# Down projections with slots on the output partitions, and experts' slots in tiles of six and four, in a macaron block of experts and attention

## The chip, the cores and the metric

The kernel runs on one core of one Trainium2 chip. The metric is the device time of one execution, in microseconds (us); lower is better. The profiles are of one execution each, taken by the hardware profiler. In them PE is TensorE (PEld its weight loads), DVE is VectorE, ACT is ScalarE, POOL is GpSimd and SP is SyncE. L12 is line 12 of the kernel file.

## The reference

x has 4 x 2048 rows (tokens) of D = 256 f32 values. The block is a "macaron": half a mixture-of-experts layer, an attention layer, and half a mixture-of-experts layer again, each on the normalized rows and added to x.

```python
x = x + 0.5 * ffn(layernorm(x), router_w, wg, wu, wd)
x = x + attn(layernorm(x), Wq, bq, Wk, bk, Wv, bv, Wo, bo)
x = x + 0.5 * ffn(layernorm(x), router_w, wg, wu, wd)

def ffn(x, router_w, wg, wu, wd):              # E = 8 experts, K = 2 of them per token, F = 1024
    capacity = int(1.25 * N / E)               # 1280 slots per expert
    topw, topi = top_k(softmax(x @ router_w.T), K)
    ...                                        # each expert keeps its `capacity` heaviest tokens
    g = einsum('ecd,edf->ecf', disp, wg)       # disp: the kept tokens' rows
    u = einsum('ecd,edf->ecf', disp, wu)
    eo = einsum('ecf,efd->ecd', silu(g) * u, wd)
    out = zeros.at[token].add(eo * weight)     # back to the tokens, scaled
```

The attention is linear: a softmax over the 16 features of each head of q, a softmax of that over the tokens for k, a context per head, and the projection Wo. Its work is not touched by the change.

## The kernel before, in words

**Stages.** The program runs through: the first router (layer norm statistics, logits, choice of two experts, a bisection for each expert's threshold, up to 96 us in the profile), the first phase of experts (to about 892 us), attention (to about 1100), the second router's threshold (to about 1169), and the second phase of experts (to the end). A phase of experts is a call of `experts`.

**An expert.** Each has 1280 slots, ten tiles of 128. Before the change they are worked in two chunks of CH = 5 tiles, 16 chunks k in a phase; k even is an expert's first chunk, k odd its second. For each chunk: `gather` fetches the rows by indirect DMAs from GpSimd's queue, one for each tile, into tiles `r`; `norm` applies the layer norm on ScalarE (L625); `turn` transposes the rows on TensorE (L636, `tr`), so that D lies on the partitions, and ScalarE copies them out (L639, `xsT`). Then `units` makes the gate and up products and `down` the down projection.

**Strassen–Winograd.** Both `units` and `down` use the seven-product scheme for a 2 x 2 block product in place of eight products. In `units` the blocks are the halves of D, the halves of F, and the halves of the slots (BH = 320 columns each). F's half is worked in NF = 4 units p of 128; each unit has seven products for the gate (m = 0) and for the up weights (m = 1), all at L701. The weights' sums `ws` are made per expert by `weight_sums` (L588), the rows' sums `xs` by `sums_of_x`. VectorE adds the products up from PSUM (L642), ScalarE takes the silu (L729, L751), and the product silu(g) * u is `finish` (L732), on VectorE for p = 0, 1 and 3 and on GpSimd for p = 2. `sums_of_h` then makes the sums of the hidden blocks that the down products need, on GpSimd (L645) for p = 0, 1 and 2 and on VectorE for p = 3. `h(p)` and `hT(p)` name the hidden blocks and their sums; they lie with F on the partitions and slots along the free dimension.

**The down projection.** `down` makes seven products over four p each (L912). In each call a 128 x 128 block of the down weights, or of their sums `wds`, is the stationary operand and 320 slots of the hidden state move, so the result has D on the partitions:

```python
nc.tensor.matmul(ps, a(p), b(p), start=(p == 0 and not more), stop=(p == NF - 1), skip_group_check=more)
```

In the call the second argument is stationary and the third moves. The result `y` must come back to slots on the partitions: `send` transposes it on TensorE (L864, `back`), ScalarE scales each row by its routing weight into a buffer `eo` (L845), and GpSimd issues one indirect DMA per tile that adds the rows into the output in DRAM (L846). A phase's last chunk takes `down_at_once` (L973): eight plain products for each tile, hidden tile stationary, 256 weight columns moving, no transposes.

**Order.** Inside `experts` the order on TensorE, VectorE, ScalarE and SP is the order in which the code issues (`tc.manual_schedule`); GpSimd's is chosen by the framework's scheduler. Work of the next chunk and expert is put between the products by hand: `early` and `late` (called in unit p of `units`), `next_list` (the row list of the next expert, made during an even chunk from 64 small products at L535 whose operands ScalarE makes at L529), `sums_of_w` (the next expert's `ws`, on VectorE during an odd chunk's `down`), and `sum_of_wd`. `gather(k + 1)` is issued in unit 0 of an odd chunk, `gather(k + 2)` in its `down`. PSUM accumulators come from `banks()`, three buffers of two banks each, reused in turn. In `down`, c11 is the first product's accumulator, p1 its copy, and u2 and u3 are partial sums.

Of the kernel before, what the change touches and what calls it, by code (L numbers as in the profile page):

```python
# [27 lines left out]
def macaron_kernel(  # L28
# [31 lines left out]
    CH = 5  # L60
# [416 lines left out]
    class RowList:  # L477
# [12 lines left out]
        def high(self):  # L490
            hi = self.pool.tile([P, T * HI], F16, tag="hi", name="hi", bufs=1)
            hv = self.pool.tile([P, 2 * T * HI], F16, tag="hv", name="hv", bufs=1)
            at = slot_hi[:, self.e, :]
            if self.waited_for:
                shape = [P, HI, T // TG, TG]
# [10 lines left out]
            else:  # L506
                shape, hi = [P, T, HI], hi.rearrange("p (t i) -> p t i", i=HI)
# [3 lines left out]
                self.hv = hv.rearrange("p (t k i) -> p t k i", k=2, i=HI)  # L511
                nc.vector.tensor_scalar(self.hv[:, :, 0, :], hi, row_in, None, ALU.mult)
                nc.vector.tensor_tensor(self.hv[:, :, 1, :], hi, spread(row_of.unsqueeze(2), shape), ALU.mult)

# [57 lines left out]
    BH = CH * P // 2  # L572
    TURN = 3
# [17 lines left out]
    def experts(name, src, dst, wait_for, rest, weights, ws, wpool, lpool, pool, ppool):  # L591
# [4 lines left out]
        PER = ST // CH  # L596
        NL = T // TG
        assert PER == 2 and ST % CH == 0
        chunks = [(e, i) for e in range(E) for i in range(0, ST, CH)]
        lists, got, xTs, turned, wds, xs = {}, {}, {}, {}, {}, {}  # L600
        sent, gathers = {-1: list(wait_for)}, {}

        def gather(k):
# [4 lines left out]
            for i in range(i0, i0 + CH):  # L608
                r = lpool.tile([P, W], F32, tag="r", name="r", bufs=10)
                gathers[k].append(nc.gpsimd.indirect_dma_start(  # L610
                    out=r, out_offset=None, in_=src[:, :],
                    in_offset=bass.IndirectOffsetOnAxis(ap=lists[e][:, i : i + 1], axis=0),
                ))
                got[k].append(r)
# [12 lines left out]
        def turn(k, q):  # L627

            if k >= len(chunks):
                return  # L630
            if q == 0:
                turned[k] = xTs[k] = pool.tile([P, DC, CH * P], F32, tag="xsT", name="xsT", bufs=2)
            c, i0, i1 = q // 2, (0, TURN)[q % 2], (TURN, CH)[q % 2]
# [13 lines left out]
        def sums_of_w(e, m):  # L647
            for _ in weight_sums(nc.vector, e, wpool, weights, ws, m):
                pass
# [25 lines left out]
        def sums_of_x(k):  # L675
            if k >= len(chunks):
                return
            v = turned.pop(k)
            o = xs[k] = pool.tile([P, 4, BH], F32, tag="xs", name="xs", bufs=1)
# [10 lines left out]
        def units(k):  # L690
            e = chunks[k][0]
# [42 lines left out]
            def first_product(p):  # L734

                ps = both(p, 0, 0, xT[:, 0, :BH])
                p1 = pool.tile([P, 2, BH], F32, tag="p1", name="p1", bufs=1)
# [3 lines left out]
            def sixth_product(p):  # L741
# [13 lines left out]
            if k == 0:  # L755

                turn(0, 1)
                cts[0] = pool.tile([P, 2, 4, BH], F32, tag="ct", name="ct", bufs=NF)
# [15 lines left out]
            send(k - 1, 2, 3)  # L774
# [67 lines left out]
        def send_tile(k, i, ps):  # L842
            e, i0 = chunks[k]
            eo = pool.tile([P, D], F32, tag="eo", name="eo", bufs=5)
            nc.scalar.mul(eo, ps, got[k][i][:, D + e : D + e + 1])  # L845
# [3 lines left out]
                in_=eo, in_offset=None, compute_op=ALU.add,  # L849
# [6 lines left out]
        def send(k, *tiles):  # L856
# [3 lines left out]
            y = ys[k]  # L860
            ps = ppool.tile([P, BANK], F32, tag="tr", name="back", bufs=1)
            for n, i in enumerate(tiles):
                for j in range(DC):
                    nc.tensor.transpose(  # L864
                        ps[:, n * D + j * P : n * D + (j + 1) * P], y[:, j, i * P : (i + 1) * P], ident
                    )
# [17 lines left out]
        def late(k, p):  # L884

            if p == 0:
                send(k - 1, 4)
# [606 lines left out]
```

## Time and profile before

| | us |
|---|---|
| median of 3 runs | 1972.2 (1971.08 to 1973.48) |
| profiled execution, its own time | 1971.7 |
| its span, from first to last instruction | 1969.7 |
| TensorE busy | 1843.7 |
| VectorE busy | 1337.3 |
| ScalarE busy | 1039.1 |
| GpSimd busy | 1027.3 |
| first phase of experts, from 96 to 892 us: TensorE busy | 784.3 of 796 |
| second phase of experts, from 1169 to 1969 us: TensorE busy | 779.4 of 800 |

How to read the profile: "busy" is the time in which at least one instruction of the engine runs. Matmuls overlap each other in the array, so the mean duration of one is longer than the distance from one start to the next; that distance is called pitch below. A line of groups reads: code line, engine, operation, output <- inputs, shape, count | busy us, mean ns of one | idle us of the engine just before them, with who ended most of that idle time. A line of the chain or of the timeline begins with the start and the length in us. The granted TensorE clock is full in the two phases of experts, except at their starts.

### The profile page before, as it was taken

The numbers are of one execution on the slowest core, as the hardware profiler recorded it, in microseconds if no ns is written. First come the engines' busy times: TensorE is split into PE (matmuls) and PEld (weight loads), VectorE is DVE, ScalarE is ACT, GpSimd is POOL, SyncE is SP. The second block draws the span as 40 slices with busy tenths as digits, with TensorE's granted clock in tenths as the row PEclk, the third lists the DMA queues.
The fourth block names the chain that finished last, engine by engine and source line by source line (L and its number), as shares of the span: only waits on it lengthen the run. The fifth ranks groups of instructions, "written<-read, shape, count | busy, mean of one in ns | idle before, by whom it ended". The sixth has DMA issues, their size and how long they took to land.

```text
span 1969.7 us, 25694 instructions
## 1 busy us (share of the span) xinstructions
PE 1843.7 (94%) x8840; PEld 1333.2 (68%) x8840; DVE 1337.3 (68%) x2445; ACT 1039.1 (53%) x2647; POOL 1027.3 (52%) x1003
## 2 busy tenths in 40 slices
PE   7389999999999999999999639999999999999998
PEld 5256677777777777777888526667777777777776
DVE  7766767676767676646677667776666767676763
ACT  5676555454646463325666368473737373737332
POOL 5245555555555555535555433555555555555552
PEclk9599999999999999999999859999999999999999
DMA  9822222222222221115012540222232313131121
GB/s 336 278 93 71 50 71 50 71 50 71 50 71 50 72 50 29 28 22 179 22 43 90 200 158 5 71 50 71 50 75 47 88 33 95 28 96 28 31 28 19
DMA packets 108002, 148.87 MB, mean 76 GB/s; under 512 B 7512, under 2 KB 94560, under 8 KB 107872
## 3 DMA queue, kind: packets, MB, share of 16 engines
q1 hardware_dynamic: 76992, 103.16, 15.3%
q0 software_dynamic: 30720, 43.93, 13.6%
q8 instruction: 70, 1.15, 0.2%
q10 hardware_dynamic: 160, 0.14, 0.1%
q14 instruction: 60, 0.49, 0.1%
HBM read 91.11 MB, written 56.10 MB: 75 GB/s over the span
## 4 chain that ended last, share of the span: by engine, by line
PE 47%; DVE 4%; issue 1%; ACT 1%; POOL 1%; DMA 1%; POOLq 0%; ACTq 0%; SPq 0%; DVEq 0%
PE mm L701 24%; PE mm L912 10%; PE py L1227 3%; PE pc L1169 3%; PE qp L1110 2%; PE back L864 1%; PE tr L636 1%; PE trq L1157 1%; PE ix L535 1%; PE trx L1102 1%; DVE above L431 1%; DVE cand L438 0%; DVE ct L642 0%; POOL out_dram L846 0%; DMA xw<-acc 0%
## 5 line engine op out<-in xcount | busy, mean ns | idle before, releaser
L701 PE MATMUL mm<-xs,ws 128*128 128x320 f32 x1536 | 477.6, 433 | 2.9 <-DVE u L642 1.8
L645 POOL TENSOR_TENSOR ct<-ct 128x320 f32<-128x320 f32 x360 | 340.4, 945 | 189.1 <-DVE ct L732 165.6
L701 PEld LDWEIGHTS mm<-xs,ws 128*128 128x128 f32 x1536 | 284.0, 190 | 112.0 <-DVE u L642 2.8
L642 DVE TENSOR_TENSOR ct<-u,mm 128x640 f32<-128x640 f32 x256 | 209.8, 820 | 177.6 <-PE mm L701 146.7
L610 POOL DMA_INDIRECT r<-rows,ixs x160 | 156.7, 980 | 280.6 <-ACT eo L845 182.1
L729 ACT ACTIVATE ct<-ct 128x960 f32<-128x960 f32 (+2 forms) x192 | 141.7, 738 | 281.9 <-DVE ct L642 276.4
L642 DVE TENSOR_TENSOR ct<-ct,mm 128x640 f32<-128x640 f32 x288 | 235.9, 819 | 74.0 <-PE mm L701 69.8
L912 PE MATMUL mm<-ct,wds 128*128 128x320 f32 x960 | 278.8, 433 | 3.4 <-DVE y L642 2.1
L529 ACT ACTIVATE lo<-from_below,behind_lo 128x129 f16<-128x129 f32 x896 | 272.9, 395 | 0.0
L912 PEld LDWEIGHTS mm<-ct,wds 128*128 128x128 f32 x960 | 179.1, 190 | 76.8 <-DVE ct L642 3.5
L912 PE MATMUL mm<-ct,wdt 128*128 128x320 f32 x720 | 213.9, 433 | 0.0
L846 POOL DMA_INDIRECT out_dram<-eo,ixs x80 | 128.5, 1606 | 144.9 <-ACT eo L845 127.0
L846 POOL DMA_INDIRECT acc<-eo,ixs x80 | 127.6, 1596 | 145.2 <-ACT eo L845 127.2
L701 PE MATMUL mm<-xsT,wgt 128*128 128x320 f32 x512 | 185.9, 445 | 0.1
L701 PE MATMUL mm<-xsT,wut 128*128 128x320 f32 x512 | 180.7, 435 | 0.0
L732 DVE TENSOR_TENSOR ct<-ct 128x640 f32<-128x640 f32 (+1 forms) x128 | 159.8, 1248 | 21.8 <-ACT ct L729 21.8
L912 PEld LDWEIGHTS mm<-ct,wdt 128*128 128x128 f32 x720 | 131.8, 190 | 47.4 <-issue 0.3
L642 DVE TENSOR_TENSOR u<-p,mm 128x640 f32<-128x640 f32 x128 | 105.1, 821 | 83.0 <-PE mm L701 66.1
L701 PE MATMUL mm<-xsT,ws 128*128 128x320 f32 x512 | 159.5, 434 | 0.0
L738 ACT COPY p<-mm 128x640 f32<-128x640 f32 x128 | 88.2, 689 | 131.5 <-PE mm L701 129.6
L845 ACT ACTIVATE eo<-back,r 128x256 f32<-128x256 f32 x150 | 64.8, 477 | 137.0 <-PE back L864 134.2
L701 PEld LDWEIGHTS mm<-xsT,wut 128*128 128x128 f32 x512 | 97.7, 191 | 40.7 <-issue 0.8
(299 smaller groups left out, 2881.8 us busy)
## 6 DMA issues: line engine op xcount, KB each, us to landing
wgt<-in_L_ffn_wg_dram SPq DMA_DIRECT2D x16, 1024.0 KB
wut<-in_L_ffn_wu_dram SPq DMA_DIRECT2D x16, 1024.0 KB
wdt<-in_L_ffn_wd_dram SPq DMA_DIRECT2D x16, 1024.0 KB
rows<-xw SPq DMA_DIRECT2D x6, 2240.0 KB
xw<-in_L_attn_x_dram SPq DMA_DIRECT2D x16, 512.0 KB
acc<-xw SPq DMA_DIRECT2D x4, 2048.0 KB
out_dram<-xw SPq DMA_DIRECT2D x16, 512.0 KB
xw<-acc SPq DMA_DIRECT2D x15, 512.0 KB
```

The source lines that it names most:

```text
L529: nc.scalar.activation(lo[:, t, :], from_below, AF.Sign, bias=at, scale=1.0)
L610: gathers[k].append(nc.gpsimd.indirect_dma_start(out=r, out_offset=None, in_=src[:, :], in_offset=bass.IndirectOffsetOnAxis(ap=lists[e][:, ...
L642: nc.vector.tensor_tensor(o, a, b, op)
L645: nc.gpsimd.tensor_tensor(o, a, b, op)
L701: nc.tensor.matmul(ps, a, b, start=start, stop=True, skip_group_check=not start)
L729: nc.scalar.activation(h(p)[:, qs, :], h(p)[:, qs, :], AF.Silu)
L732: engine.tensor_tensor(h(p)[:, qs, :], h(p)[:, qs, :], hT(p)[:, qs, :], ALU.mult)
L738: nc.scalar.copy(p1, ps)
L845: nc.scalar.mul(eo, ps, got[k][i][:, D + e : D + e + 1])
L846: ins = nc.gpsimd.indirect_dma_start(out=dst[:, :], out_offset=bass.IndirectOffsetOnAxis(ap=lists[e][:, i0 + i : i0 + i + 1], axis=0), in_ ...
L912: nc.tensor.matmul(ps, a(p), b(p), start=(p == 0 and not more), stop=(p == NF - 1), skip_group_check=more)
L1169: nc.tensor.matmul(pcs[b][:, c, 0 : D + 1], eks[i][:, k, c * P : (c + 1) * P], ring[i % 4][:, k, :], start=(first and k == 0), stop=(last ...
```

## The change

The hidden state becomes the stationary operand of the down products and the weights move, 128 slots at a time, so the result has slots on its partitions. The transposes `back` and the buffers `eo` go; ScalarE scales y's rows in place, and the scatters read y. Because each half of a chunk must then be whole tiles, an expert's ten tiles are split into six and four (SIZES) in place of five and five; the halves of `turn`, the buffers' sizes and the tiles given to each `send` follow. p1, u2 and u3 lie in hidden tiles whose first block has been read. Half of the next expert's weight sums, those of the up weights (m = 1), are issued on GpSimd, next to the first half on VectorE. In `high`, which makes operands of the row list, a scratch tile is dropped and the two products' order is exchanged.

```diff
-    CH = 5
+    SIZES = (6, 4)
...
         def high(self):
-            hi = self.pool.tile([P, T * HI], F16, tag="hi", name="hi", bufs=1)
             hv = self.pool.tile([P, 2 * T * HI], F16, tag="hv", name="hv", bufs=1)
             at = slot_hi[:, self.e, :]
...
             else:
-                shape, hi = [P, T, HI], hi.rearrange("p (t i) -> p t i", i=HI)
+                shape = [P, T, HI]
+                self.hv = hv.rearrange("p (t k i) -> p t k i", k=2, i=HI)
+                hi = self.hv[:, :, 0, :]
                 nc.vector.tensor_tensor(
                     hi, spread(count[:, :HI].unsqueeze(1), shape), spread(at.unsqueeze(2), shape), ALU.is_equal
                 )
-                self.hv = hv.rearrange("p (t k i) -> p t k i", k=2, i=HI)
-                nc.vector.tensor_scalar(self.hv[:, :, 0, :], hi, row_in, None, ALU.mult)
                 nc.vector.tensor_tensor(self.hv[:, :, 1, :], hi, spread(row_of.unsqueeze(2), shape), ALU.mult)
+                nc.vector.tensor_scalar(hi, hi, row_in, None, ALU.mult)
...
-    BH = CH * P // 2
-    TURN = 3
+    BIG = max(SIZES) * P // 2
...
-        chunks = [(e, i) for e in range(E) for i in range(0, ST, CH)]
+        assert PER == 2 and sum(SIZES) == ST and not any(n % 2 for n in SIZES)
+        chunks = [(e, sum(SIZES[:j])) for e in range(E) for j in range(PER)]
...
+        def size(k):
+            return SIZES[k % PER]
+
+        def half(k):
+            return size(k) * P // 2
+
+        def sized(k, tag, *shape, bufs=1):
+
+            n = 1
+            for m in shape:
+                n *= m
+            flat = pool.tile([P, n * BIG], F32, tag=tag, name=tag, bufs=bufs)[:, : n * half(k)]
+            letters = "abc"[: len(shape)]
+            return flat.rearrange(
+                f"p ({' '.join(letters)} s) -> p {' '.join(letters)} s", **dict(zip(letters, shape))
+            )
...
-            for i in range(i0, i0 + CH):
-                r = lpool.tile([P, W], F32, tag="r", name="r", bufs=10)
+            for i in range(i0, i0 + size(k)):
+                r = lpool.tile([P, W], F32, tag=f"r{k % PER}", name="r", bufs=size(k))
...
+            n = size(k)
             if q == 0:
-                turned[k] = xTs[k] = pool.tile([P, DC, CH * P], F32, tag="xsT", name="xsT", bufs=2)
-            c, i0, i1 = q // 2, (0, TURN)[q % 2], (TURN, CH)[q % 2]
+                turned[k] = xTs[k] = pool.tile([P, DC, n * P], F32, tag=f"xsT{k % PER}", name="xsT", bufs=1)
+            c, i0, i1 = q // 2, (0, n // 2)[q % 2], (n // 2, n)[q % 2]
...
-        def sums_of_w(e, m):
-            for _ in weight_sums(nc.vector, e, wpool, weights, ws, m):
+        def sums_of_w(engine, e, m):
+            for _ in weight_sums(engine, e, wpool, weights, ws, m):
                 pass
...
-            v = turned.pop(k)
-            o = xs[k] = pool.tile([P, 4, BH], F32, tag="xs", name="xs", bufs=1)
+            v, BH = turned.pop(k), half(k)
+            o = xs[k] = sized(k, "xs", 4)
...
-            e = chunks[k][0]
+            e, BH = chunks[k][0], half(k)
...
-                p1 = pool.tile([P, 2, BH], F32, tag="p1", name="p1", bufs=1)
+                p1 = sized(k, "p1", 2)
...
-                u2s[p] = pool.tile([P, 2, BH], F32, tag="u2", name="u2", bufs=2)
+                u2s[p] = sized(k, "u2", 2, bufs=2)
...
-                cts[p] = pool.tile([P, 2, 4, BH], F32, tag="ct", name="ct", bufs=NF)
+                cts[p] = sized(k, "ct", 2, 4, bufs=NF)
...
                 second_product(0)
-            send(k - 1, 2, 3)
+            send(k - 1, *range(size(k - 1) // 2, size(k - 1))[:2])
...
-        def send_tile(k, i, ps):
+        def send_tile(k, i, y):
             e, i0 = chunks[k]
-            eo = pool.tile([P, D], F32, tag="eo", name="eo", bufs=5)
-            nc.scalar.mul(eo, ps, got[k][i][:, D + e : D + e + 1])
+            to = ys[k][:, i * D : (i + 1) * D]
+            nc.scalar.mul(to, y, got[k][i][:, D + e : D + e + 1])
             ins = nc.gpsimd.indirect_dma_start(
                 out=dst[:, :],
                 out_offset=bass.IndirectOffsetOnAxis(ap=lists[e][:, i0 + i : i0 + i + 1], axis=0),
-                in_=eo, in_offset=None, compute_op=ALU.add,
+                in_=to, in_offset=None, compute_op=ALU.add,
...
-            y = ys[k]
-            ps = ppool.tile([P, BANK], F32, tag="tr", name="back", bufs=1)
-            for n, i in enumerate(tiles):
-                for j in range(DC):
-                    nc.tensor.transpose(
-                        ps[:, n * D + j * P : n * D + (j + 1) * P], y[:, j, i * P : (i + 1) * P], ident
-                    )
-            for n, i in enumerate(tiles):
-                send_tile(k, i, ps[:, n * D : (n + 1) * D])
-            if CH - 1 in tiles:
+            for i in tiles:
+                send_tile(k, i, ys[k][:, i * D : (i + 1) * D])
+            if size(k) - 1 in tiles:
                 del got[k], ys[k]
+
+        def outputs(k):
+            ys[k] = pool.tile([P, 2 * BIG // P * D], F32, tag="y", name="y", bufs=1)
+            return ys[k]
...
                 lists[chunks[k][0] + 1] = more.pop(0).end()
                 gather(k + 1)
             elif p == 2:
-                norm(k + 1, 0, 1, 2, 3)
+                norm(k + 1, *range(4))
             elif p == 3:
-                norm(k + 1, 4)
+                norm(k + 1, *range(4, size(k + 1)))
             if p < 3:
                 next_list(k, lows=(p,))
 
         def late(k, p):
 
             if p == 0:
-                send(k - 1, 4)
+                send(k - 1, *range(size(k - 1) // 2 + 2, size(k - 1)))
...
-            e = chunks[k][0]
-            own = pool.tile([P, 7, BH], F32, tag="y", name="y", bufs=1)
-            ys[k] = own[:, :4, :].rearrange("p (j t) s -> p j (t s)", j=DC)
-            p1, u2 = own[:, 4, :], own[:, 5, :]
+            e, n = chunks[k][0], size(k)
+            y = outputs(k)[:, : n * D].rearrange("p (t i r d) -> p t i r d", t=2, r=DC, d=P)
+            p1, u2, u3 = (hs[p][0][:, 0, :] for p in range(3))
+
+            def tiles(ap):
+                return ap.rearrange("p (i d) -> p i d", d=P)
+
+            def out_block(r, t):
+                return y[:, t, :, r, :]
...
             def product(ps, a, b, ps_of=range(NF), more=False):
-                for p in ps_of:
-                    nc.tensor.matmul(
-                        ps, a(p), b(p), start=(p == 0 and not more), stop=(p == NF - 1), skip_group_check=more
-                    )
-
-            u3 = own[:, 6, :]
+
+
+                for i in range(n // 2):
+                    s = slice(i * P, (i + 1) * P)
+                    for p in ps_of:
+                        nc.tensor.matmul(
+                            ps[:, s], b(p)[:, s], a(p), start=(i == 0 and p == 0 and not more),
+                            stop=(p == NF - 1), skip_group_check=True,
+                        )
+
+            def bank():
+                return banks()[:, 0, : n * P // 2]
+
             most, final, second = range(NF - 1), range(NF - 1, NF), k % PER == PER - 1
-            c11 = banks()[:, 0, :BH]
-            two = banks()[:, :, :BH]
+            c11 = bank()
+            two = banks()[:, :, : n * P // 2]
...
             product(two[:, 1], summed(2), hT(0), most)
             product(two[:, 0], summed(1), hT(1), most)
             if second:
-                sums_of_w(e + 1, 0)
+                sums_of_w(nc.vector, e + 1, 0)
+                sums_of_w(nc.gpsimd, e + 1, 1)
             elif e + 1 < E:
                 following[0].high()
...
             tt(u3, u2, two[:, 1], ALU.add)
             turn(k + 1, 3)
             product(c11, block(0, 1), h(2), more=True)
-            nc.scalar.copy(own[:, 0, :], c11)
+            nc.scalar.copy(out_block(0, 0), tiles(c11))
             next_list(k, lows=(6, 7))
             if second:
-                sums_of_w(e + 1, 1)
                 gather(k + 2)
-            p5 = banks()[:, 0, :BH]
+            p5 = bank()
             product(p5, summed(0), h(1))
-            tt(own[:, 3, :], u3, p5, ALU.add)
+            tt(out_block(1, 1), tiles(u3), tiles(p5), ALU.add)
             sums_of_x(k + 1)
             aside(k)
-            p4 = banks()[:, 0, :BH]
+            p4 = bank()
             product(p4, block(1, 1), hT(2))
-            tt(own[:, 2, :], u3, p4, ALU.add)
+            tt(out_block(1, 0), tiles(u3), tiles(p4), ALU.add)
             product(p5, summed(3), h(3), more=True)
-            send(k, 0, 1)
-            tt(own[:, 1, :], u2, p5, ALU.add)
+            send(k, *range(n // 2))
+            tt(out_block(0, 1), tiles(u2), tiles(p5), ALU.add)
             made = next_list(k, products=range(NL))
...
+            e, n = chunks[k][0], size(k)
+            outputs(k)
+
+            order = [(i, p, j) for i in range(n) for p in range(NF) for j in range(2)]
```

More of the change, by code (lines that the diff above doesn't have):

```diff
@@ L494, in high @@
             if self.waited_for:
+                hi = self.pool.tile([P, TG * (P + 1)], F16, tag="lo", name="hi", bufs=8)[:, : T * HI]
                 shape = [P, HI, T // TG, TG]
@@ L591, in experts @@
     def experts(name, src, dst, wait_for, rest, weights, ws, wpool, lpool, pool, ppool):
-        PER = ST // CH
+        PER = len(SIZES)
         NL = T // TG
-        assert PER == 2 and ST % CH == 0
-        chunks = [(e, i) for e in range(E) for i in range(0, ST, CH)]
+        assert PER == 2 and sum(SIZES) == ST and not any(n % 2 for n in SIZES)
+        chunks = [(e, sum(SIZES[:j])) for e in range(E) for j in range(PER)]
         lists, got, xTs, turned, wds, xs = {}, {}, {}, {}, {}, {}
         sent, gathers = {-1: list(wait_for)}, {}
+        def size(k):
[11 more added lines that the diff above has]
+            )
         def gather(k):
@@ L757, in units @@
                 turn(0, 1)
-                cts[0] = pool.tile([P, 2, 4, BH], F32, tag="ct", name="ct", bufs=NF)
+                cts[0] = sized(k, "ct", 2, 4, bufs=NF)
                 ps = banks()
@@ L962, in down_at_once @@
         def down_at_once(k, hs):
-            e = chunks[k][0]
-            order = [(i, p, j) for i in range(CH) for p in range(NF) for j in range(2)]
+            e, n = chunks[k][0], size(k)
+            outputs(k)
+            order = [(i, p, j) for i in range(n) for p in range(NF) for j in range(2)]
             order = sorted(order[: 4 * NF], key=lambda o: (o[1] == NF - 1, o[0])) + order[4 * NF :]
@@ L999, in experts @@
             rest.step()
-            norm(0, *range(TURN))
+            norm(0, *range(size(0) // 2))
             for q in (0, 2):
                 turn(0, q)
-            norm(0, *range(TURN, CH))
+            norm(0, *range(size(0) // 2, size(0)))
             for k, (e, i0) in enumerate(chunks):
                 (down if k < len(chunks) - 1 else down_at_once)(k, units(k))
-                if i0 + CH == ST:
+                if i0 + size(k) == ST:
                     load_expert(e + 2, wpool, weights)
```

## The prediction

> **What bounds the kernel now.** I read the page's shares first, then the groups of TensorE by shape, then the chain that ended last in one expert, then the timelines of TensorE and GpSimd there.
>
> ```profile
> PE 1843.7 (94%) x8840; PEld 1333.2 (68%) x8840; DVE 1337.3 (68%) x2445; ACT 1039.1 (53%) x2647; POOL 1027.3 (52%) x1003
> ```
>
> TensorE is busy 94% of the span; nothing else is near. The chain over a boundary of two chunks (a chunk is half an expert's slots) shows that it runs on TensorE alone:
>
> ```profile
> 1339.55 22.61 PE mm L701 x84
> 1362.16 0.33 PE tr L636 x3
> 1362.49 2.15 PE mm L701 x8
> 1364.64 1.61 PE mm L912 x6
> ...
> 1371.88 8.62 PE mm L912 x32
> 1380.49 0.44 PE back L864 x4
> 1380.93 3.26 PE mm L701 x12
> ```
>
> So no other engine ends a wait here, and the change is priced in TensorE passes, then checked for waits. Pitch of a pass over 320 columns: 22.61/84 = 8.62/32 = 0.269 us. A `back` transpose: 0.44/4 = 0.109 us. The groups give the counts:
>
> ```profile
> L912 PE MATMUL mm<-ct,wds 128*128 128x320 f32 x960 | 278.8, 433 | 3.4 <-DVE y L642 2.1 <-DVE ct L642 1.3
> L912 PE MATMUL mm<-ct,wdt 128*128 128x320 f32 x720 | 213.9, 433 | 0.0
> ...
> L864 PE MATMUL back<-ident,y 128*128 128x128 f32 x300 | 47.9, 273 | 1.5 <-DVE y L642 1.5
> L973 PE MATMUL mm<-wdt,ct 128*128 128x256 f32 x160 | 34.9, 379 | 0.0
> ...
> L1203 PE MATMUL ctx<-gT,wvx 128*128 128x128 f32 x32 | 4.3, 278 | 0.7 <-ACT gT L1193 0.7
> ```
>
> The means (433, 273 ns) are latencies of overlapping passes, so I use pitches. An f32 call leaves two records (7 products x 4 x 2 = 56 a chunk, x 30 chunks = 1680 = 960 + 720); a transpose leaves one. L973: 80 passes take 17.43 us in the timeline, or (17.43 - 0.38)/79 = 0.216 us each at 256 columns.
>
> **Part 1: slots on output partitions.** Removed: 300 `back` transposes, 300 x 0.109 = 32.7 us of TensorE that nothing covers. Replaced: 1680 passes of 320 columns (452.4 us) by passes over 128 columns of weights, with the hidden tile as the stationary operand. A chunk of n tiles needs 7 x 4 x (n/2) x 2 = 28n: 168 for six, 112 for four. With 16 large and 14 small chunks that is 2688 + 1568 = 4256 passes. The last chunk of each phase (`down_at_once`) now has four tiles: 128 passes of 256 columns where there were 160, 27.6 us for 34.5.
>
> The price of a 128-column f32 pass with a new stationary operand each time decides. The nearest row is the context product of attention (same type, shape and alternation):
>
> ```profile
> 997.48 1.05 PE L1203 MATMUL ctx<-gT,wvx 128*128 128x128 f32 x8
> 998.37 0.38 PE L1169 MATMUL pc<-xs,ek 128*128 128x257 f32 x1
> ```
>
> Eight passes take 0.89 us: 0.111 each. The transposes give 0.109 as the floor; the mean duration of a weight load, 190 ns, is the ceiling, if loads stopped overlapping. I take 0.111, since it is the same operation. [...]
>
> Sum: before 452.4 + 34.5 + 32.7 = 519.6; after 472.4 + 27.6 = 500.0. **-19.6 us.** Each nanosecond of pitch is 4.3 us.
>
> ScalarE's scaling now reads SBUF in place of PSUM: 477 ns (L845) against 501 (L1146, SBUF, same shape), in ScalarE's gaps; nothing. y is single-buffered and scatters read it directly, but the next write to y comes a whole up phase later (over 24 us), after scatters that end some 12 us into it; nothing. p1, u2 and u3 move into the hidden tiles' first block, whose reader c11 is done by then; nothing. The reordered `high()` is 2.9 us of VectorE in the large chunk's down phase, and costs at most 0.7 more each (487 ns becoming 1218); that phase grows from 15 to 18.6 us of TensorE, which covers it.
>
> **Part 2: six and four tiles.** Up products: 112 passes a chunk. Both widths lie on the line through 256 (0.216) and 320 (0.269), so 384 costs 0.3225, and 112 x (0.3225 + 0.216) = 60.3 us a pair, as 2 x 112 x 0.269. Nothing by itself. But TensorE's cover shrinks in the small chunk (24.2 us of up passes for 30.1) while GpSimd has fixed costs there:
>
> ```profile
> 1341.85 1.02 POOL L610 DMA_INDIRECT r<-rows,ixs  x1 [0.31 <-DVE ct L642]
> ...
> 1348.22 1.62 POOL L846 DMA_INDIRECT out_dram<-eo,ixs  x1 [0.30 <-issue]
> 1350.58 3.69 POOL L645 TENSOR_TENSOR ct<-ct 128x320 f32<-128x320 f32 x4 [0.73 <-DVE ct L732]
> 1358.11 3.69 POOL L645 TENSOR_TENSOR ct<-ct 128x320 f32<-128x320 f32 x4 [3.84 <-DVE ct L732]
> 1361.75 2.92 POOL L732 TENSOR_TENSOR ct<-ct 128x1280 f32<-128x1280 f32 x1
> ```
>
> This is the second chunk of an expert, which starts at U = 1332.88. GpSimd issues five scatters (1.57 + 0.30 us each) and five gathers (0.97 + 0.30), then the sums of h of p = 0 and 1, then the product for p = 2 (L732), ending at 1364.67; TensorE needs that for the p = 2 passes of c11, at 1364.48 + 4 x 0.269 = 1365.56. Slack 0.9 us. In the changed kernel's order GpSimd has six scatters, then six gathers, then the same sums. From U: scatters 0 to 2 go out early; scatter 3 waits for its scaling, which follows `second_product(0)` on ScalarE: about 4.3. Three scatters 5.6, six gathers 7.6: GpSimd is free at 17.5, where the first sums were ready at 13.6. Durations by 320 -> 0.92 and 1280 -> 2.91, linear: 256 -> 0.80, 1024 -> 2.4. So 17.5 + 3.2 + 3.2 + 2.4 = 26.3. TensorE wants it after 24.2 us of passes, 0.33 of `tr`, 0.11 of `ixT`, 0.2 of small waits and four passes of c11: 25.3. **TensorE waits 1.0 us** in 7 small chunks a phase: +14 us. It queues all of c11 and the two products behind it. The bounds are 0.1 (scatter 3 a microsecond earlier) and 2.0 (sums as slow as the last four of the chunk, 1.15 us each for 320 columns): 1 to 28 us. The large chunk has room: its passes grow by a fifth, GpSimd's sums less.
>
> The start of each phase waits for VectorE (0.91 us before 1184.70); its sums there grow with 384 columns. 4 x 0.07 + 2 x 0.13 = 0.5 us a phase: **+1**.
>
> **Part 3: up weights' sums for m = 1 on GpSimd.** VectorE loses four L588 of 690 ns (2.8 us) in the small chunk's down phase, which shrinks from 15.1 us to 12.4; with them it would have run late. GpSimd gains four of 1.27 us, starting when it has finished that chunk's sums, about U + 30, done by U + 36. The next chunk reads them at U + 41, and the gathers behind them wait for the scalings at U + 39 anyway. Cost nothing; if that cover went, up to 5 us each, 14 times. [...] The number of gathers and scatters (160 each) and SP's weight loads, behind each expert's last products, are as before.
>
> **Sum:** -19.6 + 14 + 1 = -4.6, on the profiled execution's 1971.7 (span 1969.7): 1967. The runs' median, 1972.2, is 0.5 above it, so the forecast stands for the median too. 0.2% is 4 us, about what a measurement of this kernel can tell from no change.
>
> **The rivals.**
> (a) GpSimd's queue isn't late: its sums at 256 columns are shorter, or scatter 3 is earlier. For it: 1.0 us is the difference of two sums of 26. Against: the order is fixed, and every term has a row. Then -18.6: 1953.
> (b) Slower: weight loads set the pitch. Nothing changes sign until the pitch is 0.1122 (4256 x 0.0011 = 4.6), and it is slower by over 0.2% from 0.1131. [...] For it: PEld already takes 190 ns a load, and 36 loads in a row are nowhere in this trace. Against: eight in a row hold 0.111.
> (c) A four-tile chunk's short groups (four passes, 0.86 us) expose latencies: ScalarE's p copy and VectorE's u at the chunk's start, silu before the next unit. I find 0.0 to 0.2 us a unit, but in small chunks GpSimd's lateness hides these, so they don't add: 1967 to 1975.
> That the change doesn't do what it says is excluded: the counts above are in its instruction order.
>
> **How the numbers follow.** As worked out, 0.45: 1967, by its bounds 1955 to 1976. (a) 0.22: 1953. (b) 0.23: 1978 to 2000 and beyond. (c) 0.10. Faster by over 0.2% (below 1968.3): 0.22 from (a), 0.30 of the likeliest, 0.03 of (c): 0.55. Slower (above 1976.1): 0.23 from (b), 0.02 from the likeliest, 0.03 from (c): 0.28. Within: 0.17. The range runs from just below (a), 1951, into (b) almost to 0.116: 1986.
>
> **What would show it.** Right: L864 gone from TensorE; 32 or more L912 passes in a row at 0.111; in small chunks a wait of about 1 us of the down matmuls on GpSimd's L732, 14 times; no wait on GpSimd's L588. Wrong: a pitch of 0.113 or more, no such wait, or waits on VectorE in small chunks' up units.

## The result: 75 us slower, and the profile after

The changed kernel takes 2046.97 us (median of 4 runs, 2044.93 to 2049.18) against 1972.49 for the kernel before on the same chip (4 runs): a ratio of 1.0378, interval 1.0360 to 1.0396. The forecast was 1967. The profiled execution's span is 2043.0 us, where it was 1969.7. The lines of the kernel have moved: L701 is now L719 (up products), L912 is L936 (down products), L732 is L750 (the product with the hidden tile's other half), L642 and L645 are L660 and L663 (sums on VectorE and GpSimd), L846 and L845 are L864 and L863 (scatter and scaling), L610 is L627 (gather), L738 is L756 (the copy of p); L588 keeps its number. `back` (L864 before) is gone.

The page's shares (busy us, share of the span, instructions):

```profile
PE 1851.3 (91%) x11084; PEld 1480.2 (72%) x11084; DVE 1399.6 (69%) x2391; ACT 1048.1 (51%) x2645; POOL 1135.1 (56%) x1059
```

Of the 73 us of span, 66 are idle time of TensorE (191.7 us for 126.0); it is also busy for 8 us more, where its passes were to take 19.6 less. VectorE has lost 54 instructions and is busy for 62 us more: its instructions got longer. The groups of TensorE by shape (busy time, mean ns | idle time ahead, and what ended it) and its waits (total, times, longest):

```profile
L936 PE MATMUL mm<-wds,ct 128*128 128x128 f32 x2432 | 301.5, 280 | 4.7 <-DVE ct L660 4.7
L936 PE MATMUL mm<-wdt,ct 128*128 128x128 f32 x1824 | 236.7, 283 | 51.5 <-POOL ct L750 28.3 <-DVE ct L660 23.2
```

```profile
PE mm L936 <- POOL ct L750: 28.3, 13, 2.3
PE mm L936 <- DVE ct L660: 28.0, 24, 2.3
PE mm L719 <- ACT p L756: 9.5, 12, 0.9
```

The first wait was forecast, at 14 us; the other two stand in no term of the forecast's sum. Together they are 65.8 us, about as much as the new idle time. The chain that ended last, over one boundary from a small chunk (four tiles) to a large one (start us, us, what):

```profile
1389.88 15.54 PE mm L719 x72
...
1406.65 1.29 DVE ct L660 x2
1407.94 0.06 DVE ct L750
1408.00 2.59 issue
...
1417.15 1.69 DVE ws L588
...
1418.87 1.74 DVE ws L588 x2
...
1422.15 0.43 DVE ct L660
...
1422.71 3.81 PE mm L936 x32
1426.52 33.64 PE mm L719 x104
...
1471.65 10.72 PE mm L936 x96
```

Before, this chain was TensorE alone. Now it leaves TensorE at 1406.65 and comes back at 1422.71: the small chunk's down phase hangs on VectorE. The last line gives the pitch of the new passes: 10.72/96 = 0.1117 us. The timeline of the same place shows what holds VectorE up:

```profile
1386.84 1.56 POOL L864 DMA_INDIRECT out_dram<-y,ixs  x1 [2.18 <-ACT y L863]
1395.05 1.83 POOL L627 DMA_INDIRECT r<-rows,ixs  x1 [0.30 <-issue]
1400.66 7.15 POOL L663 TENSOR_TENSOR ct<-ct 128x256 f32<-128x256 f32 x8
1407.78 2.33 POOL L750 TENSOR_TENSOR ct<-ct 128x1024 f32<-128x1024 f32 x1
1407.85 2.81 DVE L750 TENSOR_TENSOR ct<-ct 128x512 f32<-128x512 f32 x1
1410.17 1.16 PE L936 MATMUL mm<-wdt,ct 128*128 128x128 f32 x8 [2.25 <-POOL ct L750]
1410.58 0.68 DVE L660 TENSOR_TENSOR ct<-ct,mm 128x512 f32<-128x512 f32 x1
1411.74 0.86 DVE L750 TENSOR_TENSOR ct<-ct 128x512 f32<-128x512 f32 x1 [0.48 <-ACT ct L747]
1412.64 4.52 DVE L660 TENSOR_TENSOR ct<-ct 128x256 f32<-128x256 f32 x4
1414.02 2.86 POOL L588 TENSOR_TENSOR ws<-wut 128x512 f32<-128x512 f32 x2
1417.08 1.76 DVE L588 TENSOR_TENSOR ws<-wgt 128x512 f32<-128x512 f32 x1
...
2019.74 0.68 DVE L750 TENSOR_TENSOR ct<-ct 128x512 f32<-128x512 f32 x1
```

VectorE's L750 at 1407.85 begins 0.07 us after GpSimd's and ends 0.55 us after it. The last line is the same shape with GpSimd idle, and takes 0.68. So its work came only behind GpSimd's 2.33 us. The one at 1411.74 begins 0.31 us before the end of one of GpSimd's sums and again ends 0.55 us behind it, so it takes 0.86. L660 and L588 are longer too while GpSimd works on L663 and its new L588: the L588 at 1417.08 takes 1.76 us, where the same group took 0.68 before. An L660 that takes one of its inputs from PSUM (`mm`), like the one at 1410.58, isn't held up: in this shape 108 of them inside GpSimd's sums and products take 682 ns on average, the others 687. The means over the kernel, VectorE's groups by shape, and below them one from before:

```profile
L660 DVE TENSOR_TENSOR ct<-ct 128x256 f32<-128x256 f32 x56 | 62.9, 1124 | 1.9
L588 DVE TENSOR_TENSOR ws<-wgt 128x512 f32<-128x512 f32 x28 | 31.9, 1140 | 0.0
...
L588 DVE TENSOR_TENSOR ws<-wgt 128x512 f32<-128x512 f32 x28 | 19.1, 684 | 0.0
```

Behind TensorE's wait of 2.25 us, which ended at 1410.17, the granted clock was 0.50 for 3.41 us. Stretches of the timeline: behind the length stand the busy us (instructions) of PE, PEld, DVE, ACT and POOL, then the granted clock, the DMA share and GB/s:

```profile
1407.94:1411.35 3.41, 1.18 (x10) 1.19 (x11) 3.32 (x2) 0.06 (x1) 3.25 (x3) 1.00 1.02 414
1411.35:1414.76 3.41, 3.41 (x18) 3.41 (x17) 2.91 (x4) 0.84 (x2) 3.25 (x4) 0.50 0.12 47
...
1510.34:1513.75 3.41, 1.74 (x15) 1.74 (x16) 2.92 (x3) 0.61 (x2) 3.25 (x3) 1.00 0.97 395
1513.75:1517.16 3.41, 3.41 (x32) 3.41 (x32) 3.31 (x4) 0.79 (x3) 3.25 (x4) 1.00 0.03 5
```

The 24 passes from 1411.61 took 4.35 us, those from 1513.34, at full clock, 2.92. Apart from their starts and the end, the two phases of experts of this execution have ten stretches at half clock. Each is 3.41 us long, and their starts lie multiples of 3.41 us apart. If the phases are cut into steps of this length at the same places, TensorE was idle for 2.07 to 3.04 us in each step ahead of a half one, and in no other step for more than 1.9. The wait 102 us later is as long, 2.25 us, but lies across the border of two steps, with 1.7 us of idle time in the fuller one, and the clock behind it is 1.00.

### The profile page after: what moved, and what is told of

Same layout as the page of the kernel before. It is cut to its first block, busy times and chain, and to the rows that moved or that the text cites. A ratio compares the mean times of both kernels' runs of the same rounds, so it can differ in the third digit from the quotient of the medians.

```text
span 2043.0 us, 30241 instructions
## 1 busy us (share of the span) xinstructions
PE 1851.3 (91%) x11084; PEld 1480.2 (72%) x11084; DVE 1399.6 (69%) x2391; ACT 1048.1 (51%) x2645; POOL 1135.1 (56%) x1059
## 4 chain that ended last, share of the span: by engine, by line
PE 79%; DVE 14%; issue 3%; ACT 2%; DMA 1%; POOL 1%; ACTq 0%; POOLq 0%; DVEq 0%; SPq 0%
PE mm L719 47%; PE mm L936 18%; DVE ct L660 5%; DVE ws L588 3%; PE pc L1197 3%; PE py L1255 2%; PE qp L1138 2%; PE ix L536 1%; DVE above L431 1%; PE tr L654 1%; PE mm L1001 1%; DVE cand L438 1%; PE tr L1377 1%; DVE ct L750 1%; PE trq L1185 1%
## 5 line engine op out<-in xcount | busy, mean ns | idle before, releaser
L663 POOL TENSOR_TENSOR ct<-ct 128x384 f32<-128x384 f32 (+1 forms) x360 | 356.4, 992 | 240.5 <-DVE ct L750 216.7
L719 PE MATMUL mm<-xs,ws 128*128 128x256 f32 (+1 forms) x1536 | 479.5, 435 | 3.5 <-DVE u L660 2.1
L719 PEld LDWEIGHTS mm<-xs,ws 128*128 128x128 f32 x1536 | 286.1, 190 | 127.3 <-DVE u L660 8.3
L660 DVE TENSOR_TENSOR ct<-u,mm 128x768 f32<-128x768 f32 (+1 forms) x256 | 209.6, 819 | 167.4 <-PE mm L719 148.8
L660 DVE TENSOR_TENSOR ct<-ct,mm 128x768 f32<-128x768 f32 (+3 forms) x348 | 265.2, 762 | 75.6 <-PE mm L719 60.2
L936 PE MATMUL mm<-wds,ct 128*128 128x128 f32 x2432 | 301.5, 280 | 4.7 <-DVE ct L660 4.7
L936 PEld LDWEIGHTS mm<-wds,ct 128*128 128x128 f32 x2432 | 289.6, 196 | 7.1 <-DVE ct L660 6.0
L936 PE MATMUL mm<-wdt,ct 128*128 128x128 f32 x1824 | 236.7, 283 | 51.5 <-POOL ct L750 28.3
L627 POOL DMA_INDIRECT r<-rows,ixs x160 | 167.6, 1048 | 203.0 <-ACT y L863 104.7
L936 PEld LDWEIGHTS mm<-wdt,ct 128*128 128x128 f32 x1824 | 225.4, 198 | 60.9 <-POOL ct L750 30.8
L864 POOL DMA_INDIRECT out_dram<-y,ixs x80 | 127.6, 1595 | 145.6 <-ACT y L863 127.0
L864 POOL DMA_INDIRECT acc<-y,ixs x80 | 127.0, 1588 | 145.9 <-ACT y L863 127.3
L750 DVE TENSOR_TENSOR ct<-ct 128x1536 f32<-128x1536 f32 (+3 forms) x128 | 192.8, 1506 | 17.2 <-ACT ct L747 17.2
L719 PE MATMUL mm<-xsT,wgt 128*128 128x256 f32 (+1 forms) x512 | 184.1, 441 | 9.5 <-ACT p L756 9.5
L719 PE MATMUL mm<-xsT,wut 128*128 128x256 f32 (+1 forms) x512 | 181.0, 435 | 0.0
L756 ACT COPY p<-mm 128x768 f32<-128x768 f32 (+1 forms) x128 | 88.5, 691 | 152.5 <-PE mm L719 127.8
L719 PE MATMUL mm<-xsT,ws 128*128 128x256 f32 (+1 forms) x512 | 159.6, 434 | 0.0
L660 DVE TENSOR_TENSOR u<-p,mm 128x768 f32<-128x768 f32 (+1 forms) x128 | 104.9, 820 | 70.6 <-PE mm L719 62.3
L719 PEld LDWEIGHTS mm<-xsT,wgt 128*128 128x128 f32 x512 | 93.8, 191 | 51.1 <-ACT p L756 18.4
L719 PEld LDWEIGHTS mm<-xsT,wut 128*128 128x128 f32 x512 | 97.7, 191 | 40.7 <-issue 1.2
```

Source lines behind the costliest of these rows:

```text
L627: gathers[k].append(nc.gpsimd.indirect_dma_start(out=r, out_offset=None, in_=src[:, :], in_offset=bass.IndirectOffsetOnAxis(ap=lists[e][:, ...
L660: nc.vector.tensor_tensor(o, a, b, op)
L663: nc.gpsimd.tensor_tensor(o, a, b, op)
L719: nc.tensor.matmul(ps, a, b, start=start, stop=True, skip_group_check=not start)
L750: engine.tensor_tensor(h(p)[:, qs, :], h(p)[:, qs, :], hT(p)[:, qs, :], ALU.mult)
L756: nc.scalar.copy(p1, ps)
```

## The experiments

Theory L (lock): a VectorE instruction with two inputs in SBUF and a GpSimd one that reads SBUF exclude each other in this kernel, as the two L750 above (2.81 us for 0.68), so the up weights' sums on GpSimd, costed at nothing, slow VectorE past its slack. Its rival Q (queue): the loss is GpSimd's queue alone, late by much more than the 1.0 us forecast.

**Part 3 undone** in the changed kernel (`e1_ws_vector`).

```
-                sums_of_w(nc.gpsimd, e + 1, 1)      # in down, ahead of turn(k + 1, 1)
...
             if second:
+                sums_of_w(nc.vector, e + 1, 1)
                 gather(k + 2)
```

> Part 3 undone: the up weights' sums (L588, m = 1) are issued on VectorE again, at their old place. Theory L (lock): in the changed kernel GpSimd's two-input operations and VectorE's two-SBUF-input operations exclude each other, and the four sums on GpSimd (5.9 us instead of 5.1) stretch VectorE's sums and L588 in the small chunk's down phase; without them VectorE's L588 is back at 690 ns, and 15 to 40 of the 74 us come back: 2005 to 2032. Theory Q (queue): the loss is GpSimd's lateness from its six scatters and six gathers alone; the wait of L936 on L750 (28 us) stays, VectorE gets 2.8 us more of work in each small chunk, and the time is 2047 or up to 40 us more.

Measured: 2003.85 us, ratio 1.0163 [1.0133, 1.0192], as L has it. Of TensorE's waits the one on GpSimd's product is left, and the 28.0 us on L660 are down to 1.6. The wait, and the timeline at the place:

```profile
PE mm L936 <- POOL ct L750: 26.7, 12, 2.2
```

```profile
1387.73 2.35 POOL L750 TENSOR_TENSOR ct<-ct 128x1024 f32<-128x1024 f32 x1
1387.83 2.80 DVE L750 TENSOR_TENSOR ct<-ct 128x512 f32<-128x512 f32 x1
```

Part 3 costs 43 us here, and the queue's wait is untouched by it: two causes, not one. Even without Part 3, VectorE's L750 takes 2.80 us beside GpSimd's late product of p = 2, for 0.68 alone.

**Part 3 alone** on the kernel before (`e4_before_ws_pool`).

```
+                sums_of_w(nc.gpsimd, e + 1, 1)      # beside sums_of_w(nc.vector, e + 1, 0)
...
-                sums_of_w(e + 1, 1)
```

> Part 3 alone, on the kernel before: five and five tiles, the old down projection, the up weights' sums on GpSimd beside the gate weights' sums on VectorE. Q: GpSimd is idle there, and nothing waits for it: 1968 to 1974. L: VectorE's sums and L588 take up to twice as long, VectorE ends the small chunk's tail 1 to 3 us later, and TensorE waits for it: 1985 to 2015.

Measured: 2008.19 us, 1.0185 [1.0155, 1.0214]: 36 us slower with five-tile chunks, the old down projection and no late queue. TensorE's new waits, the first on the sums of h of p = 3 (some 1.6 us each), the second on u3:

```profile
PE mm L912 <- DVE ct L642: 25.4, 18, 2.1
PE mm L912 <- DVE y L642: 7.9, 12, 0.7
```

**GpSimd's sums replaced by fills** in the changed kernel (`e6_memset`): four instructions in the same places, which write SBUF and read nothing.

```
-                sums_of_w(nc.gpsimd, e + 1, 1)
+                for j in range(4 if e + 1 < E else 0):
+                    nc.gpsimd.memset(ws[e + 1][:, 1, j, :], 0.25)
```

> The changed kernel with GpSimd's four sums of the up weights (L588, m = 1) replaced by four memsets of the same tiles: GpSimd writes and reads nothing (these weights' sums are left out, so the up products of later experts are wrong). Theory L, if it is reading from SBUF that excludes VectorE: VectorE's sums of h and L588 in the small chunk's tail are back near 0.45 to 0.7 us, and the time is that of part 3 undone or a little less, 1992 to 2006. If GpSimd's being busy, or its writing, is what costs: 2030 to 2047.

Measured: 1995.66 us, 1.0122 [1.0102, 1.0142]. VectorE's groups, and the four fills at one place:

```profile
L660 DVE TENSOR_TENSOR ct<-ct 128x256 f32<-128x256 f32 x56 | 33.6, 600 | 1.9
L588 DVE TENSOR_TENSOR ws<-wgt 128x512 f32<-128x512 f32 x28 | 19.2, 684 | 0.0
...
1387.67 1.92 POOL L956 MEMSET ws<- 128x512 f32 x4
```

L588 is back at 684 ns and L660 at 600, from 1124. The fills are shorter than the sums (1.9 us for 5.9), so not all of VectorE's sums met them; but those that ran beside a fill and nothing else of GpSimd's, 30 of L660 and 24 of L588, took 425 and 688 ns on average, for 421 and 685 with GpSimd idle. So in this kernel VectorE's sums ran longer beside those of GpSimd's instructions that read SBUF, and not beside the fills, which write it and read nothing.

**Sizes four and six** (`e2_four_six`).

```
-    SIZES = (6, 4)
+    SIZES = (4, 6)
```

> Only SIZES is changed, to (4, 6): the second chunk of an expert, in which GpSimd has its scatters and gathers, is the large one, with eight of them in place of twelve. Both theories: GpSimd's product for p = 2 (L750) is in time, and the 28 us wait on it goes. Q: nothing else remains, so the 19.6 us of TensorE show: 1952 to 1962. L: GpSimd's L663 and L588 still meet VectorE's tail, but under a down phase of 18.7 us in place of 12.4; some of the 28 us wait on VectorE stays: 1965 to 1990.

Measured: 2039.38 us, 1.0343 [1.0313, 1.0373]; waits of 22.0 us on L750, 19.5 on L660 and 12.9 on the copy of p. I had counted wrongly: in either order the small chunk carries the large one's scatters and gathers. The run doesn't separate the theories.

**Scatters of tiles 3 to 5 of each large chunk left out** (`e3_no_late_scatters`).

```
             nc.scalar.mul(to, y, got[k][i][:, D + e : D + e + 1])
+            if k % PER == 0 and i > 2:
+                return
```

> Scatters of tiles 3 to 5 of each large chunk are left out (these rows are missing from the output): GpSimd is free about 5.6 us earlier in the small chunk, with nothing else changed. Q: the wait on L750 goes, and with it all of the loss: 1955 to 1970. L: the wait on L750 goes, and GpSimd's last sums meet less of VectorE's tail, but the up weights' sums on GpSimd still exclude VectorE's: 1975 to 2010, and VectorE's L588 stays above 1 us.

Measured: 2012.26 us, 1.0206 [1.0176, 1.0235]. The wait on L750 is gone, and what is left is VectorE:

```profile
PE mm L938 <- DVE ct L660: 41.3, 30, 2.1
```

The three scatters (5.6 us of GpSimd's queue) do make its product late, and taking them out doesn't bring the time near the forecast. Against Q as the only cause.

**Part 3 undone, and the product of p = 2 on VectorE in small chunks** (`e5_finish_vector`).

```
-                        finish(nc.gpsimd, p)
+                        finish(nc.gpsimd if k % PER == 0 or k == len(chunks) - 1 else nc.vector, p)
```

> On top of part 3 undone (2003.9 us): in small chunks the product silu(g) * u of p = 2 (L750) is made by VectorE in place of GpSimd. If the remaining loss is TensorE waiting for GpSimd's late L750 (26.7 us), and VectorE's own L750 waiting behind it (2.8 us for 0.9), most of it goes, less 1.2 us more of VectorE in its tail: 1976 to 1990. If GpSimd's lateness is not what costs, it stays at 2004 or above.

Measured: 1987.78 us, 1.0082 [1.0062, 1.0102], inside what was expected. The late product is gone; GpSimd's sums behind it are late now (9.1 us in 26 waits on L663), and the copy of p costs 12.4 us.

**Part 3 undone, and the three late scatters behind the small chunk's sums of h** (`e7_late_scatters`). y is split in two halves so that the second can wait, and p1 moves into the hidden tile for room.

```
...
+            if k % PER == 0 and i > 2:
+                held.append((k, i, to))
+            else:
+                scatter(k, i, to)
...
+            while held:                      # at the end of units(k)
+                after(scatter(*held.pop(0)), latest[-1:], "the sums of h come first")
```

> On top of part 3 undone: the scatters of tiles 3 to 5 of a large chunk are issued behind the small chunk's sums of h on GpSimd (y's second half has two buffers, p1 lies in the hidden tile to make room). GpSimd is free for the first sums about 5.6 us earlier, with the same work. Queue theory for what is left: the wait on L750 (26.7 us) goes, and VectorE's wait behind it: 1970 to 1982. If the wait only moves to VectorE's tail (sums of h of p = 3 late by the lock): 1985 to 2000.

Measured: 1977.12 us, 1.0022 [1.0009, 1.0036]. No wait on GpSimd is left; two small ones are (line numbers of this kernel):

```profile
PE mm L721 <- ACT ct L759: 10.6, 14, 0.9
PE mm L956 <- DVE y L660: 5.8, 14, 1.3
```

So lock and queue explain all but 5 us of the loss against before. The forecast saving was still nowhere to be seen. Its chain at a small chunk's start shows the first of the two waits:

```profile
1345.26 1.03 PE ix L536 x59
1346.29 2.05 PE mm L721 x8
1348.39 0.04 issue
1348.43 0.59 ACT ct L759
1349.02 0.04 issue
1349.06 1.99 PE mm L721 x8
```

**The row list's sum behind the copy of p** on ScalarE (`e8_late_scatters_sum`).

```
             first_product(0)
+            if more:
+                more[0].sum()
...
             if made:
-                made.sum()
                 more.append(made)
```

> As the late scatters, and the row list's sum (L547, ScalarE) is issued behind the copy p1 of the small chunk's first product in place of ahead of it: the wait of TensorE on ScalarE's copy L756 (9.7 us in 14 places) goes: 8 to 10 us less than the late scatters alone, and if that is at 1970 to 1978, this one beats the kernel before: 1960 to 1970.

Measured: 1980.47 us, 1.0044 [1.0027, 1.0060], with 11.2 us of the wait still there: a miss. What stands ahead of the copy on ScalarE isn't what makes it late.

**The row list's 64 products behind the first and sixth up products** (`e9_list_behind_sixth`), added to the kernel with late scatters.

```
             sixth_product(0)
+            if waiting:
+                made = waiting.pop()
+                made.begin()
+                for g in range(NL):
+                    made.products(g)
+                made.sum()
+                more.append(made)
...
-            made = next_list(k, products=range(NL))
-            if made:
-                made.sum()
-                more.append(made)
+            if k % PER == 0 and e + 1 < E:
+                waiting.append(following[0])
```

> The kernel with the late scatters (up weights' sums on VectorE, the large chunk's last three scatters behind the small chunk's sums of h), and now the row list's 64 products stand behind the small chunk's first two up products (the first and the sixth), not before them; their sum's copy on ScalarE stands behind the copy of p. Theory C (a chunk of 4 tiles has products of 256 columns, and the first and sixth products, 1.7 us, are too short a cover for the copy of p, 0.59 us behind the release and the list's copy; the list's products, 1.1 us, are cover enough): TensorE's wait for ScalarE's copy of p, 10.6 us in 14 places, falls under 2, and the time from 1977 to 1965-1969. Rival (the copy of p is late for what stands ahead of it on ScalarE, so the wait is there in any order of TensorE; or the later list makes the gathers, and the scatters behind them, late): 1974-1982.

Measured: 1958.38 us (5 runs), 0.9941 [0.9928, 0.9955] against 1971.23. Of the up products' wait on the copy of p 0.5 us is left. It brought some 18 us where 8 to 12 were expected. The stretch of the chain that holds the list's products and the first 16 passes took 5.80 us (1345.26 to 1351.06) and takes 4.69 here: 0.7 of the difference is the wait, and 0.3 are the eight passes that no longer stand right behind the list's products (1.73 us for 2.05). That is 15.5 us over 14 chunks; what the other 2 or 3 are I can't say.

**And the last two of VectorE's up weights' sums behind the write of y's fourth block** (`e10_and_sums_split`).

```
-                sums_of_w(nc.vector, e + 1, 1)
+            rest_of_w = weight_sums(nc.vector, e + 1, wpool, weights, ws, 1) if second else iter(())
+            for _ in range(2):
+                next(rest_of_w, None)            # ahead of product(p5, summed(0), h(1))
...
             tt(out_block(1, 1), tiles(u3), tiles(p5), ALU.add)
+            for _ in rest_of_w:
+                pass
```

> The same with one more step: of the four sums of the up weights on VectorE, the last two stand behind the sum that writes the fourth block of y, and no longer ahead of it. Theory: TensorE's wait for that sum, 5.8 us in 14 places (it reads the PSUM bank that the last product of the down projection adds to), goes, and nothing is late instead, since the same sums end at the same time: 4-6 us under the run with the list's products moved alone, 1959-1964 if that one is at 1965-1969. It would then be under the kernel before, 1972, by about half of the 19.6 us that the down projection's passes were to save. Rival: the last sums of the up weights, now 0.7 us later, keep the next chunk's sums of x or its sixth product waiting, and the time stays within 2 us of the run with the list's products moved alone.

Measured: 1955.32 us (5 runs, 1954.76 to 1957.65), 0.9924 [0.9910, 0.9937]: 15.9 us faster than the kernel before. The wait of 5.8 us is gone, and the time falls by 3.1 us where 4 to 6 were expected. The chain at this place is TensorE alone again:

```profile
1334.59 1.73 PE mm L721 x8
1336.32 1.03 PE ix L536 x55
...
1374.04 33.80 PE mm L721 x104
...
1431.79 1.03 PE ix L536 x58
```

A pair of chunks takes 1431.79 - 1336.32 = 95.47 us. Before it was 96.66 (between two of the lists' products, at 1331.85 and 1428.51): 1.2 us less in each of 14 pairs, 16.7 in all, about what the total says. The new passes account for 1.06 of it: 280 of 0.1117 us for 112 of 0.2693 and twenty transposes of 0.109. The late scatters and the later list were not tried on the kernel before; but there its up and down products wait for no more than 6.2 us in all.

## Why the prediction was wrong, step by step

**Part 1 was right.** `back` is gone, and the passes have a pitch of 0.1117 us in runs of 96, for 0.111 by the burst of eight in the trace of before; 4256 x 0.0007 is 3 us more than forecast. Rival (b), weight loads as the pitch, is out: no run shows the pitches of up to 0.116 and beyond to which its forecast and the range go. The -19.6 us, -16.6 at the measured pitch, are real: with no new wait left, the last kernel has 15.9 of them. Rival (a), no queue late, gave 1953, and that kernel takes 1955.

**Part 3, "Cost nothing", is the step that failed:** +43 us by undoing it, +36 by doing it alone. No term of the forecast has what the runs show of VectorE's work beside GpSimd's: 2.81 us for 0.68 in L750, 1.76 for 0.68 in L588, and 688 ns for 685 beside fills that read nothing. The trace of before had it in a row of four GpSimd sums, next to the 3.69 us of the four at 1358.11:

```profile
1364.75 4.61 POOL L645 TENSOR_TENSOR ct<-ct 128x320 f32<-128x320 f32 x4
```

Taken together they hide how much each was held up, since they only in part met VectorE's. One by one, two of the four took 1.33 us for 0.86, and VectorE's sum at 1368.67, which starts beside the last of them, 1.03 for the 0.49 of the next. But I also held that a loss of VectorE's would cost nothing, and that was an error of place. I set it against the 2.8 us that it gains and against its lead at the phase's end, the sums of x: 2.4 us, done at 1379.46 and read by TensorE at 1381.84. The timeline of before shows where the lead ends first:

```profile
1373.73 1.00 DVE L642 TENSOR_TENSOR y<-y,mm 128x320 f32<-128x320 f32 x2
1374.65 0.68 DVE L588 TENSOR_TENSOR ws<-wut 128x512 f32<-128x512 f32 x1
1376.02 2.32 PE L912 MATMUL mm<-ct,wdt 128*128 128x320 f32 x8
```

The two sums of 1373.73 are u2 and u3; they end at 1374.73, and the product p4, which waits for them (in the chain of after, the step from 1422.15 to 1422.71), starts at 1376.02: a lead of 1.3 us, not 2.4. (In 12 of 14 places of the changed kernel p4 starts 0.15 us behind u3.) The four sums that move to GpSimd (from 1374.65) stand *behind* u3 on VectorE, so taking them away does nothing for it, while what stands ahead of it gets longer beside GpSimd's. In the two timelines, after against the run with Part 3 undone, the four L660 take 4.52 for 2.62 us and two L588 1.76 and 1.64 for 0.68 and 0.69: 3.9 us lost ahead of u3, 2.6 more than the lead. p4's wait shows it: 2.3 us, or 1.2 where the clock had been at 0.50 just before (1411.36 to 1414.77). The waits on L660, 28.0 us for 1.6, are 26 of the 43. The ten stretches of half clock cost 1.7 us each (an estimate, half of 3.41), and with Part 3 undone there are two: another 14. That part hangs on chance: GpSimd's late product makes TensorE wait as long there, 12 times for up to 2.2 us, and half clock came behind two of these waits.

**Part 2, GpSimd's queue: right wait, wrong size.** The wait of the down passes on GpSimd's product was forecast at 1.0 us, 14 times, bounds 0.1 and 2.0. It is up to 2.3 us, 2.25 in the place shown, in 13 places of the records. With U at 1381.5, term by term: scatter 3 starts at U + 5.3 (4.3 forecast), because the copy of p is late on ScalarE and the scaling is behind it; GpSimd is free for the sums at U + 19.1 (17.5), one gather having taken 1.83 us for 0.95 beside VectorE's L750; the eight sums take 7.15 (6.4), also beside VectorE; the product ends at U + 28.6 (26.3). TensorE wanted it at U + 26.3 and not 25.3, as it had itself lost a microsecond at the start. And VectorE's own L750 beside it takes 2.81 us for 0.68, which I had not expected. With the late scatters no wait on GpSimd was left.

**The chunk's start, "0.2 small waits".** The copy of p takes TensorE 9.5 us in 12 small chunks. Rival (c) had named it and added that GpSimd's lateness would hide it. It did not: the copy stands at the chunk's start and the lateness at its end, and the first feeds the second through ScalarE. With four tiles the first and sixth products (1.7 us) are a short cover for the copy, and before them stood the list's products, which cover nothing there.

**The sum, as the runs give it:** -19.6 + 3 for the passes, + 28.3 + 28.0 + 9.5 for the waits is 49 of the 75 us. The rest is in TensorE's busy time. Ten stretches of half clock are 17. An estimate for 8 more: ahead of each of the 49 waits the last pass counts as busy for its whole length, some 0.17 us past the pitch (280 to 283 ns for 112). Of the three terms of the forecast, the passes were sized right, the queue's at half or less, and Part 3's was missing.

## What to carry to other kernels

Before work moves to another engine, ask which of the engine's outputs is waited for first, and count only what stands ahead of that one: the gain of this move lay behind it, and the loss ahead. Look in the trace at what two engines' instructions take beside each other: here a two-input sum from SBUF on VectorE (L588) took 1.76 us for 0.68 beside GpSimd's sums, and moving four from one to the other cost 36 to 43 us. And a smaller chunk shortens the cover of the waits in it (eight up passes take 1.73 us with four tiles, 2.58 with six, in the last kernel's chain); find for each the work that can be put behind it, as the list's products were here.

## What was not expected of the hardware

- VectorE's product of 128x512 took 2.81 us behind GpSimd's 2.33, and 0.68 alone; beside GpSimd's fills the sums were as fast as alone (688 ns for L588), and so were those with one input in PSUM beside GpSimd's sums (682 ns for 687).
- GpSimd's work was longer beside VectorE's as well: eight GpSimd sums took 7.15 us for some 6.4, and the issue of one gather on GpSimd 1.83 us for 0.95, beside VectorE's product of 1.22.
- In the changed kernel's phases of experts half clock came in steps of 3.41 us, behind steps in which TensorE had been idle for 2.07 to 3.04 us. Of two waits of 2.25 us, the one with 2.2 us in one step, at 1408, had it behind it; the one with 1.7 in the fuller of two, at 1510, had not.
- Passes right behind 64 short f16 products ran late: 2.05 us for eight that take 1.73 elsewhere, and 1.92 where the list stands later. The profile shows no wait there.
